# A recurrence's inner steps redistributed: accumulating transfers, a spectrum computed twice, a new order of steps

## The chip, the cores and the metric

One core of a Trainium2 chip runs the whole program. The metric is the device time of one execution in microseconds (us). The core's engines work side by side, each through its own queue in order: TensorE (PE, matrix products into PSUM), VectorE (DVE), ScalarE (ACT, functions from tables), GpSimd (POOL, which also issues transfers) and SyncE (SP, which only issues transfers). Both kinds of transfers run on the core's 16 DMA engines.

## The reference

An image of 256 x 256 pixels with 128 channels in float32 goes through four layers; each takes a group norm of the image and adds its result to it. The first layer is an attention along rows, the third a triangle product, the fourth a 3x3 convolution. The change lies in the second, a recurrence with 64 complex channels:

```python
mag = jnp.sqrt(Ar ** 2 + Ai ** 2 + 1e-08)
scale = 0.95 * jax.nn.sigmoid(mag) / (mag + 1e-08)
Ar = Ar * scale
Ai = Ai * scale
...
Bx_r = Br * x_r - Bi_ * x_i
Bx_i = Br * x_i + Bi_ * x_r
inp_r = delta[..., :c] * input_gate[..., :c] * Bx_r
inp_i = delta[..., c:] * input_gate[..., c:] * Bx_i
...
def step(h_state, _):
    h_r, h_i = h_state
    Ah_r = Ar * h_r - Ai * h_i
    Ah_i = Ar * h_i + Ai * h_r
    return ((fg_r * Ah_r + inp_r, fg_i * Ah_i + inp_i), None)
...
(h_r, h_i), _ = jax.lax.scan(step, h0, None, length=T)
```

A and B are the two-dimensional Fourier transforms of 7x7 complex filters, forget gate, input gate and delta come from products of the normalised image with 128x128 weights, and T is 16. The step is linear with a 2x2 matrix for each pixel and channel, so that 16 steps have a closed form in the matrix's trace and determinant.

## The kernel before, in words

The stages run one after another: statistics, attention, recurrence (the function `recurrence`), triangle, convolution. The recurrence takes the image in 64 blocks of 1024 pixels. A block's tiles have 128 partitions (64 channels for each of two halves of the block) and are 512 wide (`thin`) or 2 x 512 wide (`wide`, real and imaginary part). For every block these steps run, each a small function named in the table `order`:

- `ld` loads the pixels twice in two layouts (`xf`, `xc`) and the rows of both filters' transforms (`hs`, eight small transfers) on SP's queue.
- `za` and `zb` make the spectra of A and B from `hs` on TensorE into PSUM; `zd`, `zf`, `zi` are the three gates' products. They share two PSUM buffers of two banks each (tag `z`).
- `a2` squares the spectrum of A on ScalarE, `m2` adds the two squares with TensorE by means of the identity into PSUM (tag `s`), `lm`, `mg`, `lb`, `iv`, `sg` and `s` make the factor `scale` from it. `zaa` copies the spectrum into the SBUF tile `ar`.
- `f`, `ig`, `ae`, `al_`, `q`, `qg` are the gates' functions; `p0`, `p1`, `bx` and `v` make the input term.
- `ff`, `pf`, `t`, `d_`, `D_` give determinant and trace; `tq`, `dn`, `tr` and `u` with 2, 4, 8, 16 double the number of steps; `pf`, `t`, `u2` and `t1` are products on POOL, `u4` and `u8` on VectorE.
- `y0` and `y1` multiply `ar` with `v` on VectorE, `av` combines them with TensorE (PSUM tag `y`), `yf` and `yb` finish that part. `ac1` and `ac2` add both results onto `xc` by transfers that accumulate, issued by POOL.
- `ev_` and `bn` sum the result and its square over each block on ScalarE (into `parts`) for the next group norm; `st` writes `xc` to memory on POOL's queue.

`order` lists each step with a lag: in round `it` the step works on block `it - lag`, so that up to five blocks are in work at once. `pin` (`keep_in_program_order`) holds a step behind the instruction traced before it on its engine; the loads of `ld` are not pinned. Tiles are taken from rings of `bufs` buffers, and a buffer is written again only when its readers are done. Helpers record most instructions, so many steps have one line in the profile: L995 is a VectorE tensor-tensor, L1001 a scalar-tensor-tensor, L998 a product on POOL, L55 ScalarE, L61 TensorE.

After the last block 56 short products keep TensorE going (`warm`), `parts` is reduced, and the triangle stage begins with `tap_products` (nine 128x128 products of the convolution's taps with its dense weights) and `group_affine` (scale and shift of the group norm from the sums).

Of the kernel before, what the change touches and what calls it, by code (L numbers as in the profile page):

```python
# [31 lines left out]
class Kernel:  # L32
# [50 lines left out]
    def group_affine(self, pool, psum, stats, tag, shift=None, mv=None, busy=8):  # L83

        nc, V = self.nc, self.nc.vector
        pin = self.tc.keep_in_program_order
        pm = psum.tile([P, 2], F32, name=f"pm{tag}", tag="gn")
        d, v, mg, sd = (pool.tile([P, 1], F32, name=f"{n}{tag}") for n in ("gd", "gv", "mg", "sd"))
        if mv is None:
            mv = pool.tile([P, 2], F32, name=f"mv{tag}")  # L90
            V.tensor_reduce(mv, stats, AX.X, ALU.add)
            self.keep_busy(psum, busy)
            pin(self.mm(pm, self.g4n, mv))
            self.keep_busy(psum, 3)
# [812 lines left out]
    def recurrence(self, x1T, x2T, HD_, stats1, shift1, stats2, shift2):  # L907
# [7 lines left out]
        with ExitStack() as c:  # L915
# [58 lines left out]
            def load(b):  # L974
# [7 lines left out]
                d["hs"] = self.first_rows if b == 0 else self.row_transforms(io.tile([P, 2, HC], F32, name="hs", bufs=2), HD_, b)  # L982
# [34 lines left out]
            def total(d, name, pairs):  # L1017

                n = len(pairs)
                z = d[name] = ps.tile([P, n, 512], F32, name=name, tag="y" if n == 2 else "s", bufs=1 if n == 2 else 2)  # L1020
# [25 lines left out]
            def ab(d): halves(d, wide(d, "az"), "d", "zd", AF.Identity)  # L1046
            def ae(d): act(wide(d, "ex"), d["az"], AF.Sigmoid, scale=-1.0)
            def al_(d): act(d["ex"], d["ex"], AF.Ln, bias=1e-37)
            def q(d): stt(wide(d, "q", 2), d["ex"], -1.0, d["az"], MUL, MAX)

            def sg(d): act(d["mag"], d["mag"], AF.Sigmoid)
            def s(d): tt(thin(d, "s", 3), d["mag"], d["inv"], MUL)
# [3 lines left out]
            def ig(d): halves(d, wide(d, "ig"), "i", "zi", AF.Sigmoid)  # L1056
            def zaa(d): act(wide(d, "ar", 2), d["za"].rearrange("p r i v -> p i r v"), AF.Copy)
# [3 lines left out]
            def t(d): gt(thin(d, "t", 3), d["fs"], d["ar"][:, 0], MUL)  # L1061
            def d_(d): tt(thin(d, "d"), d["m2"][:, 0], d["ff"], MUL)
# [26 lines left out]
            def u4(d): tt(thin(d, "u4"), d["u2"], d["tr4"], MUL)  # L1089
            def tq8(d): squared(d, "tq8", "tr4")  # L1090
            def dn8(d): squared(d, "dn8", "dn4", 2)
# [3 lines left out]
            def xa(d): stt(thin(d, "g", 2), d["t"], -2.0, d["u8"], ADD, MUL)  # L1095
# [32 lines left out]
            def ev_(d): statistic(d, 0, AF.Identity)  # L1128
            def bn(d): statistic(d, 1, AF.Square, shifted=True)
            def st(d):  # L1130
                b = d["b"]
                for half in range(2):
                    dst = x2T[:, b * 1024 + half * 512:b * 1024 + (half + 1) * 512]
                    pin(nc.gpsimd.dma_start(dst.rearrange("(r c) n -> c r n", c=HC), d["xc"][half * HC:(half + 1) * HC]))
            def ld(d): load(d["b"])
# [16 lines left out]
            warm = ps.tile([P, 1, 512], F32, name="warm", tag="s")  # L1152
            for _ in range(56):
                pin(self.mm(warm[:, 0, :P], self.ident, self.cmat))
            red = wp.tile([P, 2, 2], F32, name="partsum")
            V.tensor_reduce(red, parts, AX.X, ADD)
            pr = ps.tile([P, 2], F32, name="partps", tag="s")
            for ri in range(2):
                self.mm(pr[ri * HC:(ri + 1) * HC], fold, red[:, :, ri])
            V.tensor_copy(stats2[:, :, 0], pr)  # L1160

    def triangle(self, x2T, x3T, znT, prodD, rs2D, rs3D, stats2, shift2, stats3, shift3, prepare):
# [368 lines left out]
    def tap_products(self, ps):  # L1531

        W, V = self.weights, self.nc.vector
        kt, wd = W["kt"], W["wd"]
        pb = ps.tile([P, 2], F32, name="cpb", tag="gn")
        self.mm(pb[:, 0:1], wd, W["bv"])
        V.tensor_copy(W["bw"], pb[:, 0:1])
        for t in range(3):
            pk = ps.tile([P, 3, P], F32, name="cpk")
            for n in range(3):  # L1540
                self.mm(pk[:, n], kt[:, 3 * t + n, :], wd)
            V.tensor_copy(kt[:, 3 * t:3 * t + 3, :], pk)
# [178 lines left out]
    def run(self, ctx):  # L1721
# [10 lines left out]
        stats["2"] = const.tile([P, 2, 1], F32, name="stats2")  # L1732
        shift2 = const.tile([P, 1], F32, name="shift2")
# [87 lines left out]
```

## Time and profile before

| What | us |
|---|---|
| median of 3 runs | 4684.48 |
| range of the runs | 4682.95 to 4684.81 |
| profiled execution | 4678.77 |
| its span | 4677.0 |
| first and last `za` in it | 1649.8 and 2909.7 |
| `partsum`, the recurrence's last reduction | 2973.1 |

Over the whole span TensorE is busy 97%, VectorE 80%, ScalarE 71% and POOL 45%. These are averages over four different stages. Busy time of TensorE is modelled, and the durations of matrix products overlap, so their sum is more than the time that they take; the same holds to a smaller degree for VectorE and ScalarE, whose instructions overlap by some 70 to 90 ns. Where a step's cost in a full queue is wanted, the distance from its start to the next start is the better number.

### The profile page before, as it was taken

The page shows a single profiled execution, that of the slowest core. Times are in us where ns is not written, and L with a number is a line of the kernel's source. Part 1 is how long each engine was busy: PE and PEld are TensorE (multiplying, and loading weights), DVE is VectorE, ACT ScalarE, POOL GpSimd, SP SyncE. Part 2 cuts the span into 40 slices and gives each one's busy share as a digit, 9 for nine tenths or more (in the row PEclk, how much of TensorE's full clock was granted, in tenths as well). Part 3 has the DMA queues.
Part 4 walks back from the last instruction along what each step waited for, and adds up shares of the span by engine and source line. Part 5 has one row for each costly group of instructions (what it writes and reads, how often), then busy time and mean ns, then how long its engine had stood idle before and what let it go on. Part 6 is the DMA issues. An engine that isn't in the chain of part 4 may idle for free. (4 is left out here: it accounts for less than half of the span.)

```text
span 4677.0 us, 79571 instructions
## 1 busy us (share of the span) xinstructions
PE 4521.0 (97%) x30445; PEld 2600.4 (56%) x30445; DVE 3750.3 (80%) x4827; ACT 3333.0 (71%) x5173; POOL 2101.5 (45%) x1379
## 2 busy tenths in 40 slices
PE   8999999999999989999999999899999999999999
PEld 2444555555555533333333333456999973379999
DVE  7776777777777679999999999787666677789885
ACT  7556888888888889999999999798443454442110
POOL 1333555555555547667666667333231245520000
PEclk9999999999999999999999999999999999999999
DMA  9892122222222235555555555576667758955432
GB/s 316 327 357 110 54 83 82 87 82 82 85 88 82 69 88 132 134 133 130 134 130 133 136 129 126 184 253 246 243 222 262 251 211 327 360 208 174 135 114 72
DMA packets 219655, 768.19 MB, mean 164 GB/s; under 512 B 58443, under 2 KB 60620, under 8 KB 178926
## 3 DMA queue, kind: packets, MB, share of 16 engines
q1 hardware_dynamic: 153976, 465.15, 29.2%
q0 software_dynamic: 65232, 297.90, 22.2%
q8 instruction: 244, 4.00, 0.3%
q14 instruction: 139, 1.14, 0.1%
q10 hardware_dynamic: 64, 0.00, 0.0%
HBM read 431.32 MB, written 265.55 MB: 149 GB/s over the span
## 5 line engine op out<-in xcount | busy, mean ns | idle before, releaser
L629 DVE TENSOR_TENSOR e<-sc,bT 128x1024 f32<-128x1024 f32 x512 | 613.8, 1220 | 255.8 <-PE sc L61 254.8
L629 POOL TENSOR_TENSOR ks<-e 128x1024 f32<-128x1024 f32 x256 | 602.4, 2371 | 443.2 <-PE nd L61 429.9
L55 ACT ACTIVATE e<-e 128x1024 f32<-128x1024 f32 x512 | 539.3, 1053 | 40.3 <-DVE e L629 30.7
L61 PE MATMUL m<-U,v 128*128 128x128 f32 x4608 | 514.8, 275 | 1.5 <-DVE v L1656 1.5
L61 PEld LDWEIGHTS m<-U,v 128*128 128x128 f32 x4608 | 514.6, 192 | 1.7 <-DVE v L1656 1.7
L61 PEld LDWEIGHTS z<-wf,zt 128*128 128x128 f32 x4096 | 462.6, 192 | 53.6 <-DVE LR L1169 28.0
L61 PE MATMUL z<-wf,zt 128*128 128x128 f32 x4096 | 474.8, 277 | 5.6 <-DVE LR L1169 5.5
L1169 DVE TENSOR_TENSOR LR<-z,sg 128x512 f32<-128x512 f32 (+1 forms) x323 | 270.0, 867 | 165.3 <-ACT sg L55 165.3
L1169 POOL TENSOR_TENSOR zt<-zt,df 128x512 f32<-128x512 f32 x127 | 161.5, 1271 | 423.2 <-ACT df L55 423.2
L55 ACT ACTIVATE sg<-z 128x512 f32<-128x512 f32 (+1 forms) x323 | 160.7, 509 | 243.7 <-PE z L61 241.4
L61 PE MATMUL sc<-proj 32*128 32x256 f32 x4096 | 300.5, 404 | 3.2 <-DVE e L629 2.4
L998 POOL TENSOR_TENSOR fs<-f 128x512 f32<-128x512 f32 x64 | 176.4, 2756 | 275.1 <-DVE f L995 251.1
L61 PEld LDWEIGHTS sc<-proj 32*128 32x128 f32 x4096 | 188.5, 185 | 161.8 <-PE px L61 94.8
L61 PE MATMUL nd<-e,proj 128*32 128x256 f32 x4096 | 273.7, 385 | 2.6 <-DVE og L629 2.6
L55 ACT ACTIVATE dn<-dn 128x512 f32<-128x512 f32 x384 | 237.9, 620 | 12.5 <-DVE dn L629 8.5
L1696 ACT COPY m4s<-m 128x512 f32<-128x512 f32 x32 | 18.7, 585 | 304.3 <-PE m L61 304.3
L61 PE MATMUL z<-LR 128*128 128x256 f32 x1024 | 225.5, 383 | 7.5 <-DVE LR L1169 7.5
L998 POOL TENSOR_TENSOR u<-t,tr 128x512 f32<-128x512 f32 x64 | 225.6, 3525 | 11.9 <-DVE tr L1001 10.1
L998 POOL TENSOR_TENSOR t<-t,v 128x1024 f32<-128x1024 f32 x63 | 206.9, 3285 | 50.2 <-DVE t L995 49.5
L1706 POOL DMA_DIRECT2D out_dram<-ys x32 | 37.0, 1157 | 420.9 <-DVE ys L1704 420.9
L61 PEld LDWEIGHTS z<-LR 128*128 128x128 f32 x1024 | 196.6, 192 | 35.5 <-DVE LR L1169 8.3
L1169 POOL TENSOR_TENSOR zt<-ga,zt 128x1024 f32<-128x1024 f32 x62 | 144.7, 2353 | 118.5 <-DVE ga L1169 118.5
(430 smaller groups left out, 10738.4 us busy)
## 6 DMA issues: line engine op xcount, KB each, us to landing
zt<-znT SPq DMA_DIRECT2D x96, 1024.0 KB
zt<-x2T SPq DMA_DIRECT2D x64, 1024.0 KB
xin<-in_x_dram SPq DMA_DIRECT2D x48, 1024.0 KB
xr<-x3T SPq DMA_DIRECT2D x46, 768.0 KB
x1T<-x POOLq DMA_DIRECT2D x64, 512.0 KB, 5.0
xf<-x1T SPq DMA_DIRECT2D x64, 512.0 KB
xc<-x1T SPq DMA_DIRECT2D x128, 256.0 KB
x2T<-xc POOLq DMA_DIRECT2D x128, 256.0 KB, 3.7
```

Of the source, the lines that this page charges most:

```text
L55: return self.nc.scalar.activation(out, in_, func, bias=bias, scale=scale, **kw)
L61: return self.nc.tensor.matmul(out, lhsT, rhs, start=start, stop=stop)
L629: pin = lambda f: lambda *a, **k: tc.keep_in_program_order(f(*a, **k))
L998: pin(nc.gpsimd.tensor_tensor(out, a, b_, op))
L1169: pin = lambda f: lambda *a, **k: tc.keep_in_program_order(f(*a, **k))
L1696: nc.scalar.copy(m4, m[4])
L1706: nc.gpsimd.dma_start(out[row:row + 8].rearrange("r p t c -> p (r t) c"), ys.rearrange("p g k t c -> p (g k t) c"))
```

## The change

The sum of the two squares (`m2`) is made by a transfer that accumulates one half of `a2` onto the other (by VectorE for the first block); `lm` and `d_` read it in SBUF. `ev_` becomes a transfer that accumulates `xc` onto one tile `summed`, except in the last block; `summed` is reduced once at the end. The spectrum of A is made a second time (`zc`), two rounds after `za`, and `y0` and `y1` read it in PSUM; `zaa` copies only the real part. `u4` goes from VectorE to POOL, and so does the last block's `t1`. `st` goes from POOL's queue to SP's. Short products (`f1`, `f2`, three a round) stand beside the two spectra of A. Buffers of several tiles change in number: `hs` has three instead of two; PSUM tag `s` one instead of two, with one bank for the short products. The lags and the order of all steps are new. `tap_products` runs in round 2 of the recurrence, pinned, and the group means for the next norm come from the same place as the sums (`means2`).

```diff
+            spare = ps.tile([P, 512], F32, name="spare", bufs=1)
+
+            def awake(n):
+                for _ in range(n):
+                    pin(self.mm(spare[:, :P], self.ident, self.cmat))
+
             parts = wp.tile([P, 2, 2, NB], F32, name="parts2")
+            V.memset(parts, 0.0)
+            summed = io.tile([P, 2, 512], F32, name="summed", bufs=1)
+            nc.gpsimd.memset(summed, 0.0)
...
+            folded = wp.tile([P, HC], F32, name="folded")
+            V.tensor_tensor(folded, self.g4n[:, :HC], self.g4n[:, HC:], ADD)
...
-                d["hs"] = self.first_rows if b == 0 else self.row_transforms(io.tile([P, 2, HC], F32, name="hs", bufs=2), HD_, b)
+                d["hs"] = self.first_rows if b == 0 else self.row_transforms(io.tile([P, 2, HC], F32, name="hs", bufs=3), HD_, b)
...
-            def a2(d): act(rows(wide(d, "a2")), d["za"], AF.Square)
-            def m2(d): total(d, "m2", [[(self.ident, d["a2"][:, 0]), (self.ident, d["a2"][:, 1])]])
-            def lm(d): act(thin(d, "mag"), d["m2"][:, 0], AF.Ln, bias=1e-8)
+            def a2(d): act(rows(wide(d, "a2", 2)), d["za"], AF.Square)
+            def m2(d):
+                if d["b"]:
+                    pin(nc.gpsimd.dma_start(d["a2"][:, 0], d["a2"][:, 1], accum_op=ADD))
+                else:
+                    tt(d["a2"][:, 0], d["a2"][:, 0], d["a2"][:, 1], ADD)
+            def lm(d): act(thin(d, "mag"), d["a2"][:, 0], AF.Ln, bias=1e-8)
...
-            def zaa(d): act(wide(d, "ar", 2), d["za"].rearrange("p r i v -> p i r v"), AF.Copy)
+            def zaa(d): act(thin(d, "ar", 2).rearrange("p (r v) -> p r v", v=N), d["za"][:, :, 0], AF.Copy)
...
-            def t(d): gt(thin(d, "t", 3), d["fs"], d["ar"][:, 0], MUL)
-            def d_(d): tt(thin(d, "d"), d["m2"][:, 0], d["ff"], MUL)
+            def t(d): gt(thin(d, "t", 3), d["fs"], d["ar"], MUL)
+            def d_(d): tt(thin(d, "d"), d["a2"][:, 0], d["ff"], MUL)
...
-            def u4(d): tt(thin(d, "u4"), d["u2"], d["tr4"], MUL)
+            def u4(d): gt(thin(d, "u4"), d["u2"], d["tr4"], MUL)
...
-            def y0(d): tt(wide(d, "y0"), d["ar"], both(d["v"][:, 0]), MUL)
-            def y1(d): tt(wide(d, "y1"), d["ar"], both(d["v"][:, 1]), MUL)
+            def zc(d): spectrum(d, 0, "zc")
+            def turned(d, n, k):
+                v = d["v"][:, k].rearrange("p (r v) -> p r v", v=N).unsqueeze(2).to_broadcast([P, 2, 2, N])
+                tt(rows(wide(d, n)), d["zc"], v, MUL)
+            def y0(d): turned(d, "y0", 0)
+            def y1(d): turned(d, "y1", 1)
...
-            def t1(d): (tt if last(d) else gt)(wide(d, "t1"), both(d["t"]), d["v"], MUL)
+            def t1(d): gt(wide(d, "t1"), both(d["t"]), d["v"], MUL)
...
-            def ev_(d): statistic(d, 0, AF.Identity)
+            def ev_(d):
+                if last(d):
+                    statistic(d, 0, AF.Identity)
+                else:
+                    pin(nc.gpsimd.dma_start(summed, d["xc"], accum_op=ADD))
...
-                    pin(nc.gpsimd.dma_start(dst.rearrange("(r c) n -> c r n", c=HC), d["xc"][half * HC:(half + 1) * HC]))
+                    pin(nc.sync.dma_start(dst.rearrange("(r c) n -> c r n", c=HC), d["xc"][half * HC:(half + 1) * HC]))
+            def f1(d): awake(2)
+            def f2(d): awake(1)
...
-                (e_, 3), (ld, 0), (za, 0), (u4, 2), (zb, 1), (a2, 0), (av, 2), (t, 1), (p1, 1), (zaa, 0), (m2, 0),
-                (tq8, 2), (al, 3), (zd, 0), (ev_, 4), (lD, 2), (q, 1), (yf, 2), (p0, 1), (tq2, 1), (dn2, 1), (tr2, 1),
-                (eD, 2), (tr8, 2), (lm, 0), (dn8, 2), (mg, 0), (ab, 0), (t1, 3), (qg, 1), (lb, 0), (tq16, 2), (bx, 1),
-                (ac1, 3), (iv, 0), (u8, 2), (yb, 3), (zf, 0), (sg, 0), (tq4, 1), (v, 1), (y1, 1), (f, 0), (xa, 2),
-                (D_, 1), (s, 0), (u2, 1), (ac2, 3), (tr4, 1), (ae, 0), (fs_, 0), (zi, 0), (y0, 1), (ff, 0), (pf, 0),
-                (xb, 2), (ig, 0), (be, 2), (al_, 0), (bn, 4), (d_, 0), (dn4, 1), (st, 4),
+                (ld, 0), (f1, 0), (za, 0), (a2, 0), (f2, 2), (zc, 2), (m2, 0), (bx, 2), (zaa, 0), (ac2, 4), (u2, 2), (dn8, 3),
+                (pf, 1), (v, 2), (tq16, 3), (xb, 3), (t, 1), (tq4, 2), (y1, 2), (zd, 0), (ae, 1), (dn2, 2), (lD, 2),
+                (ab, 0), (y0, 2), (be, 3), (zb, 1), (ff, 1), (eD, 2), (av, 2), (tq2, 1), (lm, 0), (mg, 0), (e_, 3),
+                (tr4, 2), (al, 3), (zi, 0), (p0, 1), (dn4, 2), (lb, 0), (p1, 1), (al_, 1), (iv, 0), (u4, 2), (yf, 2),
+                (ig, 0), (t1, 3), (d_, 1), (tq8, 2), (yb, 3), (zf, 0), (tr2, 1), (q, 1), (f, 0), (tr8, 2), (qg, 1),
+                (ac1, 3), (u8, 2), (sg, 0), (s, 0), (D_, 1), (bn, 4), (xa, 2), (ev_, 4), (st, 4), (fs_, 0),
...
+                if it == 2:
+                    self.tap_products(ps)
...
+            awake(56)
+            V.tensor_reduce(parts[:, 0, :, 0:1], summed, AX.X, ADD)
             red = wp.tile([P, 2, 2], F32, name="partsum")
             V.tensor_reduce(red, parts, AX.X, ADD)
...
+            pr = ps.tile([P, 2, 2], F32, name="partps", tag="s", bufs=1)
+            for n, m in enumerate((folded, fold)):
+                for ri in range(2):
+                    pin(self.mm(pr[ri * HC:(ri + 1) * HC, n], m, red[:, :, ri]))
+            awake(3)
+            means = self.means2
+            V.tensor_copy(means, pr[:, 0])
+            V.tensor_copy(stats2[:, :, 0], pr[:, 1])
...
-                self.tap_products(ps0)
-                ab, mg, _ = self.group_affine(wp, ps0, stats2, "2", shift=shift2, busy=0)
+                ab, mg, _ = self.group_affine(wp, ps0, stats2, "2", shift=shift2, means=self.means2)
```

More of the change, by code (lines that the diff above doesn't have):

```diff
@@ L79, in load, with group_affine @@
         return t
-    def group_affine(self, pool, psum, stats, tag, shift=None, mv=None, busy=8):
+    def group_affine(self, pool, psum, stats, tag, shift=None, mv=None, busy=8, means=None):
         nc, V = self.nc, self.nc.vector
         pin = self.tc.keep_in_program_order
-        pm = psum.tile([P, 2], F32, name=f"pm{tag}", tag="gn")
+        pm = None if means is not None else psum.tile([P, 2], F32, name=f"pm{tag}", tag="gn")
         d, v, mg, sd = (pool.tile([P, 1], F32, name=f"{n}{tag}") for n in ("gd", "gv", "mg", "sd"))
         if mv is None:
[L90 to L94, printed above, removed]
+            if means is None:
+                mv = pool.tile([P, 2], F32, name=f"mv{tag}")
+                V.tensor_reduce(mv, stats, AX.X, ALU.add)
+                self.keep_busy(psum, busy)
+                pin(self.mm(pm, self.g4n, mv))
+                self.keep_busy(psum, 3)
+            else:
+                pm = means
             V.tensor_tensor(d, pm[:, 0:1], shift, ALU.add)
@@ L1019, in total @@
                 n = len(pairs)
-                z = d[name] = ps.tile([P, n, 512], F32, name=name, tag="y" if n == 2 else "s", bufs=1 if n == 2 else 2)
+                z = d[name] = ps.tile([P, n, 512], F32, name=name, tag="y" if n == 2 else "s", bufs=1)
                 for i, terms in enumerate(pairs):
@@ L1045, in zd, with ab, q, s @@
             def zd(d): gate(d, "d")
-            def ab(d): halves(d, wide(d, "az"), "d", "zd", AF.Identity)
+            def ab(d): halves(d, wide(d, "az", 2), "d", "zd", AF.Identity)
             def ae(d): act(wide(d, "ex"), d["az"], AF.Sigmoid, scale=-1.0)
             def al_(d): act(d["ex"], d["ex"], AF.Ln, bias=1e-37)
-            def q(d): stt(wide(d, "q", 2), d["ex"], -1.0, d["az"], MUL, MAX)
+            def q(d): stt(wide(d, "q"), d["ex"], -1.0, d["az"], MUL, MAX)
             def sg(d): act(d["mag"], d["mag"], AF.Sigmoid)
-            def s(d): tt(thin(d, "s", 3), d["mag"], d["inv"], MUL)
+            def s(d): tt(thin(d, "s"), d["mag"], d["inv"], MUL)
             def zf(d): gate(d, "f")
@@ L1055, in zi, with ig @@
             def zi(d): gate(d, "i")
-            def ig(d): halves(d, wide(d, "ig"), "i", "zi", AF.Sigmoid)
-            def zaa(d): act(wide(d, "ar", 2), d["za"].rearrange("p r i v -> p i r v"), AF.Copy)
+            def ig(d): halves(d, wide(d, "ig", 2), "i", "zi", AF.Sigmoid)
+            def zaa(d): act(thin(d, "ar", 2).rearrange("p (r v) -> p r v", v=N), d["za"][:, :, 0], AF.Copy)
             def fs_(d): tt(d["f"], d["f"], both(d["s"]), MUL)
@@ L1082, in tq2, with dn2, u2 @@
             def tq2(d): squared(d, "tq2", "t")
-            def dn2(d): squared(d, "dn2", "d", 2)
+            def dn2(d): squared(d, "dn2", "d")
             def tr2(d): stt(thin(d, "tr2"), d["d"], -2.0, d["tq2"], MUL, ADD)
-            def u2(d): gt(thin(d, "u2", 2), d["t"], d["tr2"], MUL)
+            def u2(d): gt(thin(d, "u2"), d["t"], d["tr2"], MUL)
             def tq4(d): squared(d, "tq4", "tr2")
@@ L1088, in tr4, with dn8 @@
             def tr4(d): stt(thin(d, "tr4"), d["dn2"], -2.0, d["tq4"], MUL, ADD)
-            def u4(d): tt(thin(d, "u4"), d["u2"], d["tr4"], MUL)
+            def u4(d): gt(thin(d, "u4"), d["u2"], d["tr4"], MUL)
             def tq8(d): squared(d, "tq8", "tr4")
-            def dn8(d): squared(d, "dn8", "dn4", 2)
+            def dn8(d): squared(d, "dn8", "dn4")
             def tr8(d): stt(thin(d, "tr8"), d["dn4"], -2.0, d["tq8"], MUL, ADD)
@@ L1094, in tq16, with xa @@
             def tq16(d): squared(d, "tq16", "tr8")
-            def xa(d): stt(thin(d, "g", 2), d["t"], -2.0, d["u8"], ADD, MUL)
+            def xa(d): stt(thin(d, "g"), d["t"], -2.0, d["u8"], ADD, MUL)
             def last(d): return d["b"] == NB - 1
@@ L1127, in statistic @@
                     act(junk, d["xc"][:, ri], func, accum_out=parts[:, k, ri, b:b + 1], **({"bias": shiftc[:, ri:ri + 1]} if kw else {}))
-            def ev_(d): statistic(d, 0, AF.Identity)
+            def ev_(d):
+                if last(d):
+                    statistic(d, 0, AF.Identity)
+                else:
+                    pin(nc.gpsimd.dma_start(summed, d["xc"], accum_op=ADD))
             def bn(d): statistic(d, 1, AF.Square, shifted=True)
@@ L1151, in recurrence @@
                         step(D[it - lag])
-            warm = ps.tile([P, 1, 512], F32, name="warm", tag="s")
-            for _ in range(56):
-                pin(self.mm(warm[:, 0, :P], self.ident, self.cmat))
+            awake(56)
+            V.tensor_reduce(parts[:, 0, :, 0:1], summed, AX.X, ADD)
             red = wp.tile([P, 2, 2], F32, name="partsum")
             V.tensor_reduce(red, parts, AX.X, ADD)
[L1157 to L1160, printed above, removed]
+            pr = ps.tile([P, 2, 2], F32, name="partps", tag="s", bufs=1)
[6 more added lines that the diff above has]
+            V.tensor_copy(stats2[:, :, 0], pr[:, 1])
     def triangle(self, x2T, x3T, znT, prodD, rs2D, rs3D, stats2, shift2, stats3, shift3, prepare):
@@ L1531, in tap_products @@
     def tap_products(self, ps):
-        W, V = self.weights, self.nc.vector
+        W, pin = self.weights, self.tc.keep_in_program_order
         kt, wd = W["kt"], W["wd"]
-        pb = ps.tile([P, 2], F32, name="cpb", tag="gn")
-        self.mm(pb[:, 0:1], wd, W["bv"])
-        V.tensor_copy(W["bw"], pb[:, 0:1])
+        pb = ps.tile([P, 2], F32, name="cpb", tag="s", bufs=1)
+        pin(self.mm(pb[:, 0:1], wd, W["bv"]))
+        pin(self.nc.vector.tensor_copy(W["bw"], pb[:, 0:1]))
         for t in range(3):
-            pk = ps.tile([P, 3, P], F32, name="cpk")
+            pk = ps.tile([P, 3, P], F32, name="cpk", tag="s", bufs=1)
             for n in range(3):
-                self.mm(pk[:, n], kt[:, 3 * t + n, :], wd)
-            V.tensor_copy(kt[:, 3 * t:3 * t + 3, :], pk)
+                pin(self.mm(pk[:, n], kt[:, 3 * t + n, :], wd))
+            pin(self.nc.vector.tensor_copy(kt[:, 3 * t:3 * t + 3, :], pk))
     def transformed_taps(self, late):
@@ L1732, in run @@
         stats["2"] = const.tile([P, 2, 1], F32, name="stats2")
+        self.means2 = const.tile([P, 2], F32, name="means2")
         shift2 = const.tile([P, 1], F32, name="shift2")
```

## The prediction

> **What bounds the kernel now.** I read the page's slices first, then the engines by stretches, then the recurrence's groups, waits and order of time. The blocks of the recurrence fill 1650 to 2974 us. Inside it:
>
> ```profile
> core 0: us, PE busy (x) PEld busy (x) DVE busy (x) ACT busy (x) POOL busy (x), PEclk, DMA share, GB/s
> 2200.00:2400.00 200.00, 189.24 (x574) 66.21 (x572) 198.61 (x250) 198.91 (x339) 136.30 (x80) 1.00 0.56 133
> ```
>
> ScalarE and VectorE are both over 99% busy and TensorE's granted clock is 1.00, so no single engine can be relieved with profit; POOL has about 6 us free per block. ScalarE does not appear at all in the list of who waited for whom. One block lasts 20.16 us: ScalarE's Square of `za` starts at 2108.41 and, ten blocks on, at 2310.01. ScalarE's queue of work is therefore the bound, and VectorE is just behind. The groups that the change touches (busy, mean ns, idle before):
>
> ```profile
> L998 POOL TENSOR_TENSOR u<-t,tr 128x512 f32<-128x512 f32 x10 | 35.4, 3544 | 0.3
> L998 POOL TENSOR_TENSOR t<-t,v 128x1024 f32<-128x1024 f32 x10 | 33.0, 3300 | 7.0 <-DVE t L995 7.0
> L998 POOL TENSOR_TENSOR fs<-f 128x512 f32<-128x512 f32 x10 | 27.8, 2784 | 41.6 <-DVE f L995 41.6
> L995 DVE TENSOR_TENSOR y<-ar,v 128x1024 f32<-128x1024 f32 x20 | 24.4, 1222 | 0.3
> L995 DVE TENSOR_TENSOR q<-q,ig 128x1024 f32<-128x1024 f32 x10 | 15.4, 1542 | 0.0
> L998 POOL TENSOR_TENSOR t<-fs,ar 128x512 f32<-128x512 f32 x10 | 13.0, 1300 | 0.1
> L1134 POOL DMA_DIRECT2D x2T<-xc x20 | 13.0, 656 | 0.0
> L55 ACT ACTIVATE x2q<-xc 128x512 f32<-128x512 f32 x20 | 12.5, 627 | 0.3
> L55 ACT ACTIVATE ar<-za 128x1024 f32<-128x1024 f32 x10 | 10.1, 1013 | 0.0
> ```
>
> The odd thing is POOL: one 128x512 product takes 1.30 us and another of the same size 3.54. The order of time explains it:
>
> ```profile
> 2215.49 4.48 POOL L998 TENSOR_TENSOR u<-t,tr 128x512 f32<-128x512 f32 x1
> ...
> 2215.88 1.22 DVE L995 TENSOR_TENSOR q<-q,ig 128x1024 f32<-128x1024 f32 x1
> 2217.01 0.68 DVE L995 TENSOR_TENSOR u<-u,tr 128x512 f32<-128x512 f32 x1
> 2217.62 1.22 DVE L995 TENSOR_TENSOR yf<-yf,g 128x1024 f32<-128x1024 f32 x1
> 2218.75 1.21 DVE L1001 SCALAR_TENSOR_TENSOR v<-q,bx 128x1024 f32<-128x1024 f32 x1
> ...
> 2920.45 1.65 POOL L998 TENSOR_TENSOR u<-t,tr 128x512 f32<-128x512 f32 x1
> 2920.88 2.30 DVE L995 TENSOR_TENSOR q<-q,ig 128x1024 f32<-128x1024 f32 x1
> ```
>
> While VectorE runs instructions with both inputs in SBUF (`q`, `u`, `yf`), POOL's product stands; it ends with `v`, whose second input `bx` is in PSUM, so its own work is about 1.25 us. The last two lines are the opposite case: POOL got in first and VectorE's `q*ig` took 2.30 instead of 1.22. [...]
>
> **The change, part by part, per block.** Steps are counted start to start, since the instructions overlap.
>
> *ScalarE.* `ev_` (two reductions of `xc` with their reads) goes: in the order of time they take 2211.55 to 2212.92, 1.37 us. `zaa` halves: from 0.91 start to start to 0.52, the step of the other 512-wide ones, -0.39. `lm` reads SBUF instead of PSUM: 575 against 624 ns for `mag<-mag`, +0.04. The two table loads stay (the new order still goes once to the logarithms and once to the sigmoids). 20.16 - 1.37 - 0.39 + 0.04 = 18.44 us.
>
> *VectorE.* Its own work in one undisturbed block is `v` to `v`, 2199.10 to 2218.75: 19.65 us in 25 instructions; the rest to 20.16 is `q*ig` being locked out (1542 against 1219 ns) and small waits. `u4` leaves: 0.61. `y0` and `y1` now read `zc` from PSUM in a broken pattern. No row shows this: below, `v` with one PSUM input (1211) against `y` (1222) gives -0.01 each; above, `p` with PSUM in rows of 256 (740) against a plain 512 (684) gives +0.11 for twice the width. I take +0.05 each. `d_` from SBUF instead of PSUM is equal (680 against 684). 19.65 - 0.61 + 0.1 = 19.14 us: the new bound.
>
> *TensorE.* By starts, before: three gates of 1.77, `pxb` 2.77, `av` 3.6, `bx` 3.6, `m2` 1.9, and `za` with `zb` together 1.3 to 2.1 = 18.7 or more. `m2` goes (-1.9); `zc` comes at about 0.95 (as `za` alone, 2909.55 to 2910.50, before `zb`), and `za`, `zb`, `zc` no longer run side by side (+0.4); three 128-wide fillers add about 0.6. Sum 18.75, so TensorE hides only 0.4 us below VectorE.
>
> *A ring through both.* `xb`'s third product waits for `tq16` on ScalarE, `zd` stands behind it, and `ab` on ScalarE waits for `zd`. From `tq16`'s end: 0.95 + 2.0 = 3.0; from `ab` on to the next `tq16`: 18.44 less `tq4`, `ae`, `dn2`, table load and `lD` (3.9) = 14.5. Together 17.5, under the bound. The second spectrum takes TensorE's buffers in turn (`za`, `zd`, `zi` one, `zc`, `zb`, `zf` the other), and each earlier reader (`zaa`, `ab`, `ig`; `y0`, `p1`, `f`) stands ahead in the order; a stall would come only if `y0` or `p1` is late, and then VectorE is the late one anyway.
>
> *POOL.* The transfers `m2` (0.66, as another of 256 KB, to 0.9) and `ev_` (0.9) come, the two `st` (1.3) leave for SP, `u4` comes. [...] By the mean of the rows `u4` costs POOL up to 3.5 us: 14.1 + 3.5 + 1.7 - 1.3 = 18.0. [...] The new order forms two such stretches: `v`, `y1`, `y0`, `be` (1.24 + 1.14 + 1.14 + 0.6 = 4.1 us) for `u2`, `pf`, `t` (3.9), and `p0`, `p1`, `yf` (3.8) for `u4`, `t1` (1.25 + 2.37, the mean of the attention's 128x1024 product on POOL = 3.6). They fit with 0.2 us each, so some blocks miss. I charge half of what is lost today in `q*ig`, 0.16: 19.3 us.
>
> *Behind POOL's waits.* `m2` on POOL waits for `a2`, and `ac2`, `u2`, `pf`, `t` are queued behind it; `tq2` on ScalarE and then `tr2` wait for `t`. With ScalarE 0.7 us short of work it runs early: `a2` can end 2.5 us ahead of `v`, the two issues take 1.7, so POOL is in place. `lm` wants `m2` landed some 6 us after its issue; 512 KB land in 4.4 to 7.2, 256 KB of `x2T` in 3.7. Uncovered, a late landing would stop ScalarE, which has the 0.7 to give.
>
> *DMA.* One 512 KB accumulation keeps the 16 engines 2.65 us (47.3% of 5.6 us in a stretch of the drain that holds one alone). `ev_` adds 2.65 and `m2` 1.33 to today's 0.56 x 20.16 = 11.3: 15.3 of 19.3, 79%. [...] Queue by queue (39.0 and 17.2% now, `st` being 1.8 us) POOL's would only go to about 51%[...]. Landings get longer; `ac2` has 6.2 us behind `ac1` where 20 of 63 waited at about 4.5.
>
> A `yf` buffer is written again some 10 us after `ac2` is issued; a landing beyond 10 would stop VectorE.
>
> *SP.* 8 `hs` at 0.80, `xf` 0.34, two `xc` 1.35, and now `st` 1.35 = 9.4 us per block, under 19. `hs` in three buffers is released by `zc`, as now by `zb`, early in the block before its use.
>
> *Ends.* `tap_products` leaves the gap between stages: there the chain from `partsum` to `pc` takes 7.1 us (2973.08 to 2980.21), of which `pm` waited until 2978.36. About 3.5 goes; the reduction of `summed` (1024 elements) adds 1.1; inside the fill the nine products and three copies cost 0 to 3, I take 1.5. The accumulation for the last block but one no longer stands in ScalarE's tail, -1. The longer lags (`v`, `y0`, `y1`, `be`, `ff`, `tr4`, `d_` one round later) move 5.9 us of VectorE's work from the fill to the drain; the drain has holes on VectorE (`t` at 2954.16 came after POOL had been idle 6.4 us), so I take 0, with 5 either way. Together -2.
>
> **Sum.** 20.16 - 19.3 = 0.86 us over 60 full blocks (63 starts follow one another, the first few were shorter already) = 52, and 2 at the ends: -54. The profiled execution took 4678.8 (span 4677.0), so 4625; the median lies 5.7 above it, so 4630.
>
> **Rivals.** *POOL misses its stretches.* One lock-out of 1.1 us (2.30 against 1.22) in most blocks gives 19.14 + 0.6 to 1.0 = 19.7 to 20.15, that is 4654 to 4683. For it: margins of 0.2 us. Against: a miss repeats only if POOL stays late.
>
> *SP puts `st` before the loads (slower).* `st` is pinned and waits for `ac2` landed; if the next block's loads stand behind it, there is a ring: `za` 0.95, `a2` 1.06, `m2` 0.8, `ac2` issue to landing 5.0, `st` 1.35, `xf` and `xc` 1.7, eight `hs` 6.7, their landing about 3 (estimate, from 3.0 to 5.4 for the loads and stores of `xc`) = 20.6 us, +0.44 x 63 = +28: about 4710, more if the fuller DMA engines stretch it. It decides from the point where `hs` is issued over 6 us after its buffer is free. Against: the loads are not pinned, and today they do run ahead, with `hs` between `xf` and `xc`.
>
> *POOL's ring (slower).* If `u2`, `pf`, `t` keep 3.54, 2.78 and 1.30, then `tq2` to the end of the next `a2` on ScalarE (18.44 less the 7.1 of `zaa`, `dn8`, `tq16`, `tq4`, `ae`, `dn2`, a table load, `lD`, `ab`, `eD` that stand between = 11.3) plus `m2`, `ac2` (1.7) plus these 7.6 is 20.6 us: again about 4710.
>
> *The order does not do what it says*: TensorE's 18.75 with 0.5 us of waits would be 19.3, inside my forecast.
>
> **How the numbers follow.** Forecast (19.05 to 19.55) 0.68, 4607 to 4646; missed stretches 0.15, 4646 to 4690; the two rings 0.17, 4694 to 4760. The low end is 19.02 (`y` at its lower bound, no lock-out) with -6 at the ends. The range 4606 to 4690 holds some 0.8. Within 0.2% (9 us, about what a measurement can tell) lies only the far part of the missed stretches, 0.05; faster 0.78, slower 0.17.
>
> **What would show it.** A block of 19.1 to 19.5 us; VectorE over 98% busy, ScalarE about 95%; `y` at 1.21 to 1.33; `u4` and `u2` near 1.3; `q*ig` near 1.22; `za` never waiting for `hs`. Wrong if ScalarE waits for `t` or `m2`, if SP's loads wait behind `st`, or if `y` takes over 1.4.

## The result, and the profile after

The changed kernel takes 4721.86 us (median of 4 runs, 4712.70 to 4727.87) against 4684.65 for the kernel before on the same chip: 1.0082 times as long, 95% interval [1.007, 1.0094]. It is slower, by 37 us, and the prediction said 54 faster. The profiled execution took 4727.87 us, its span 4725.7.

First the slices by engine, for the same stretch as before (columns: sum, TensorE, its weight loads, VectorE, ScalarE, POOL, granted clock, DMA share, GB/s):

```profile
2200.00:2400.00 200.00, 200.00 (x627) 74.48 (x626) 187.18 (x235) 182.54 (x297) 111.37 (x89) 0.96 0.80 168
```

ScalarE came down from 198.91 to 182.54, as was meant; POOL came down from 136.30 to 111.37 although it got a product more; DMA rose from 0.56 to 0.80. But VectorE, which was to be the new bound, is at 187.18, TensorE at 200.00, and the granted clock is no longer 1.00. The groups that answer to those of before (busy, mean ns, idle before). The lines of the program have moved: L1009, L1015 and L1012 are what L995, L1001 and L998 were.

```profile
L1012 POOL TENSOR_TENSOR t<-t,v 128x1024 f32<-128x1024 f32 x10 | 23.8, 2378 | 0.0
L1009 DVE TENSOR_TENSOR y<-zc,v 128x1024 f32<-128x1024 f32 x19 | 22.4, 1218 | 0.3
L1012 POOL TENSOR_TENSOR u<-t,tr 128x512 f32<-128x512 f32 x10 | 19.4, 1940 | 0.0
L1012 POOL TENSOR_TENSOR fs<-f 128x512 f32<-128x512 f32 x10 | 19.1, 1912 | 0.0
L1012 POOL TENSOR_TENSOR u<-u,tr 128x512 f32<-128x512 f32 x10 | 16.6, 1663 | 31.4 <-DVE tr L1015 31.4
...
L1009 DVE TENSOR_TENSOR q<-q,ig 128x1024 f32<-128x1024 f32 x10 | 12.1, 1213 | 0.0
...
L55 ACT ACTIVATE ar<-za 128x512 f32<-128x512 f32 x10 | 5.9, 586 | 0.0
```

Every product on POOL is shorter than before (3300 to 2378, 3544 to 1940, 2784 to 1912), and VectorE's `q*ig` is no longer locked out (1542 to 1213). The part of the change that deals with POOL and VectorE works. The loss is on TensorE. The waits from 1800 to 2900 us name it:

```profile
engine line waited for: us in total, times, longest us
...
ACT az L55 <- PE zd L61: 98.2, 54, 2.6
...
DVE v L1015 <- PE bx L61: 69.4, 53, 2.1
```

VectorE's `v` waits for `bx` in nearly every block, ScalarE's `az` for `zd`. A steady block (from one Square of `za` to the next) takes either 19.53 or 21.23 us. Here is TensorE at the start of a long one (start, us, engine, line, operation, count):

```profile
2185.26 0.71 PE L61 MATMUL spare<-cmat,ident 128*128 128x128 f32 x4
2185.90 1.13 PE L61 MATMUL za<-ev,hs 14*128 14x512 f32 x4
2186.96 0.49 PE L61 MATMUL spare<-cmat,ident 128*128 128x128 f32 x2
2187.39 1.13 PE L61 MATMUL zc<-ev,hs 14*128 14x512 f32 x4
2188.45 1.58 PE L61 MATMUL bx<-p,scaledr 128*128 128x512 f32 x2
2189.82 1.91 PE L61 MATMUL bx<-p,scaledn 128*128 128x512 f32 x2
2191.53 1.46 PE L61 MATMUL bx<-p,scaledi 128*128 128x512 f32 x2
2192.83 1.02 PE L61 MATMUL bx<-p,scaledr 128*128 128x512 f32 x2
```

The products of `bx`, all alike, take 1.58, 1.91 and 1.46 us, and then 1.02. The slices of the same moment, with the clock in the third column from the right, say why:

```profile
2188.00:2188.50 0.50, 0.50 (x5) 0.05 (x1) 0.50 (x2) 0.50 (x2) 0.00 (x0) 1.00 0.71 147
2188.50:2189.00 0.50, 0.50 (x4) 0.26 (x3) 0.50 (x2) 0.47 (x2) 0.00 (x0) 0.99 1.00 238
2189.00:2189.50 0.50, 0.50 (x2) 0.30 (x1) 0.50 (x2) 0.50 (x3) 0.00 (x0) 0.50 1.15 287
...
2191.00:2192.00 1.00, 1.00 (x2) 0.35 (x2) 0.85 (x1) 1.00 (x3) 1.00 (x3) 0.50 0.56 189
2192.00:2192.50 0.50, 0.50 (x2) 0.12 (x1) 0.00 (x0) 0.50 (x2) 0.50 (x2) 0.60 1.07 184
2192.50:2193.00 0.50, 0.50 (x3) 0.26 (x2) 0.00 (x0) 0.50 (x1) 0.50 (x2) 1.00 1.07 188
```

For about 3.4 us (2189.0 to 2192.4) the granted clock is 0.50, directly after two spectra of 14 rows that stand together, and although TensorE is never idle. That costs 3.4 x 0.5 = 1.7 us, just what the long blocks are longer by.

Two spectra together are not enough for that, however. In the kernel before, `zb` stands directly behind `za` in 18 of the 64 blocks, and the clock stays at 1.00 there:

```profile
2183.82 1.13 PE L61 MATMUL za<-ev,hs 14*128 14x512 f32 x4
2184.77 1.20 PE L61 MATMUL zb<-ev,hs 14*128 14x512 f32 x4
2185.89 1.13 PE L61 MATMUL av<-y,ident 128*128 128x512 f32 x2
```

The slices of the same moment:

```profile
2182.65:2186.06 3.41, 3.41 (x12) 1.03 (x11) 3.41 (x5) 3.38 (x5) 2.04 (x1) 1.00 0.85 211
2186.06:2189.47 3.41, 3.41 (x8) 1.27 (x8) 3.41 (x7) 3.38 (x7) 3.28 (x4) 1.00 0.42 91
```

What differs is what stands beside them: products over 128 rows there, fillers here. How much of each stood there is counted below, in the part on why the prediction was wrong.

The profiled execution's 49 us by stretch (start of `a2` to start of `a2`, after less before):

| stretch | before | after | difference |
|---|---|---|---|
| start of the program to the first `a2` | 1651.6 | 1654.4 | +2.8 |
| first five blocks | 94.0 | 106.1 | +12.1 |
| next 58 blocks | 1169.2 | 1187.2 | +18.0 |
| last `a2` to the triangle's `pc` | 65.4 | 77.4 | +12.0 |
| `pc` to the end | 1696.8 | 1700.7 | +3.9 |

The 58 blocks at 19.53 would have been 36.5 shorter than at 20.16; the 54.5 us above that are 32 times 1.70.

### The profile page after: what moved, and what is told of

Same layout as the page of the kernel before. It is cut to its first block, busy times and chain, and to the rows that moved or that the text cites. A ratio compares the mean times of both kernels' runs of the same rounds, so it can differ in the third digit from the quotient of the medians.

```text
span 4725.7 us, 80279 instructions
## 1 busy us (share of the span) xinstructions
PE 4624.3 (98%) x30831; PEld 2665.9 (56%) x30831; DVE 3696.4 (78%) x4766; ACT 3236.9 (68%) x4921; POOL 1953.6 (41%) x1443
## 5 line engine op out<-in xcount | busy, mean ns | idle before, releaser
L1728 ACT COPY m4s<-m 128x512 f32<-128x512 f32 x32 | 18.7, 586 | 304.6 <-PE m L61 304.6
L1055 POOL DMA_DIRECT2D a<-a x63 | 53.9, 855 | 400.2 <-ACT a L55 393.2
L61 PE MATMUL av<-y,ident 128*128 128x512 f32 x384 | 193.3, 612 | 0.8 <-DVE y L1009 0.8
L1012 POOL TENSOR_TENSOR u<-u,tr 128x512 f32<-128x512 f32 x64 | 106.0, 1656 | 203.4 <-DVE tr L1015 203.4
```

The source lines that it names most:

```text
L61: return self.nc.tensor.matmul(out, lhsT, rhs, start=start, stop=stop)
L1012: pin(nc.gpsimd.tensor_tensor(out, a, b_, op))
L1055: pin(nc.gpsimd.dma_start(d["a2"][:, 0], d["a2"][:, 1], accum_op=ADD))
L1728: nc.scalar.copy(m4, m[4])
```

## The experiments

Theory: two bare spectra side by side bring the clock down, and the changed kernel is bound by TensorE. Rivals: TensorE is full whatever its clock; or VectorE, POOL or a transfer sets the block. Each edit is against the changed kernel unless another is named, and each ratio is to the kernel before on the same chip. A "filler" is one of the steps `f1` (two short products) and `f2` (one).

**The second spectrum apart from the first.** Only the place of `zc` in TensorE's order changes:

```diff
-                (ld, 0), (f1, 0), (za, 0), (a2, 0), (f2, 2), (zc, 2), (m2, 0), (bx, 2), (zaa, 0), ...
+                (ld, 0), (f1, 0), (za, 0), (a2, 0), (f2, 2), (m2, 0), (bx, 2), (zc, 2), (zaa, 0), ...
```

> The changed kernel with the second spectrum of A (zc) moved on TensorE from beside za to behind bx; the short products stay. Theory A (clock): za, zc and the short products beside them are a stretch of 3.2 us in which TensorE's products have 14 rows or are short; [...] the granted clock falls to 0.50 for 3.4 us and the block takes 21.2 instead of 19.5 us. Apart, no half-clock stretches are left, every block takes 19.5 us and the time is 4722 - 33 x 1.7 = about 4665. Rival B (the clock falls because TensorE is never idle): the half-clock stretches stay wherever the spectra stand, 4715 to 4728.

Measured: 4662.06, ratio 0.9964 [0.9952, 0.9977] to the kernel before. All blocks take 19.52.

```profile
2200.00:2400.00 200.00, 200.00 (x657) 72.54 (x655) 197.92 (x247) 189.32 (x306) 116.53 (x93) 1.00 0.84 178
```

The instructions are the same, TensorE is as full as in the changed kernel, and the clock is 1.00. By the two ratios 1.2% of the time, 55 us, hang on where four short products stand. It also shows what TensorE's work is at full clock: 19.52 per block, not 18.75.

**No fillers.** The steps `f1` and `f2` are taken out; the spectra stay together.

```diff
-                (ld, 0), (f1, 0), (za, 0), (a2, 0), (f2, 2), (zc, 2), (m2, 0), ...
+                (ld, 0), (za, 0), (a2, 0), (zc, 2), (m2, 0), ...
```

> The changed kernel without the short products f1 and f2 beside the two spectra. TensorE's own sum falls from 19.5 to 18.45 us. Theory A[...]: the bare spectra (2.1 us side by side) are weaker still and the half clock comes in as many blocks or in every one, 18.45 + 1.0 to 1.7 = 19.5 to 20.15 us, 4665 to 4702. Theory A, if the short products only lengthen the weak stretch: no half clock, VectorE bounds at 19.1 to 19.3, 4640 to 4652. Rival B (the clock falls because TensorE is never idle): TensorE gets holes, the half clock goes, 4640 to 4652 as well, but then the run with zc apart keeps its half clock.

Measured: 4785.81, ratio 1.0224 [1.0205, 1.0243], slower than any expectation. Of the 58 steady blocks 51 now have half clock, 33 of them for 3.4 us and 18 for 6.8:

```profile
2206.74 1.67 PE L61 MATMUL zc<-ev,hs 14*128 14x512 f32 x4 [0.48 <-ACT f L55]
2208.34 2.08 PE L61 MATMUL bx<-p,scaledr 128*128 128x512 f32 x2
2210.21 1.91 PE L61 MATMUL bx<-p,scaledn 128*128 128x512 f32 x2
2211.91 1.91 PE L61 MATMUL bx<-p,scaledi 128*128 128x512 f32 x2
2213.62 1.22 PE L61 MATMUL bx<-p,scaledr 128*128 128x512 f32 x2
```

So the fillers, in the place of waits, do hold the clock up (0.96 in 2200 to 2400 with them, 0.91 without), only not enough. TensorE also had to wait beside the spectra here (0.38 us before `za`, 0.48 for `f`), so this run alone does not say whether idle time or thin rows did it.

**Thin fillers.** The same fillers over the 14 rows that a spectrum uses instead of 128:

```diff
-            def awake(n):
+            def awake(n, rows_of=P):
...
-                    pin(self.mm(spare[:, :P], self.ident, self.cmat))
+                    pin(self.mm(spare[:, :P], self.ident[:rows_of], self.cmat[:rows_of]))
...
-            def f1(d): awake(2)
-            def f2(d): awake(1)
+            def f1(d): awake(2, 2 * KS)
+            def f2(d): awake(1, 2 * KS)
```

> The changed kernel with the short products f1 and f2 made over 14 rows instead of 128: the same number of products, the same columns and the same 19.5 us for TensorE, the spectra side by side as in the change. Theory A [...]: the short products no longer count, half clock in nearly every block, 4760 to 4790 as without them. Rival (every moment with a product running counts as busy): as the changed kernel, 4712 to 4728.

Measured: 4770.11, ratio 1.0172 [1.0148, 1.0197], with half clock in 48 of the 58 blocks.

```profile
2200.00:2400.00 200.00, 196.69 (x593) 74.54 (x593) 177.70 (x224) 172.62 (x282) 102.46 (x83) 0.90 0.77 162
```

As many instructions, with 14 rows, hardly hold the clock: 0.90 here, 0.96 with 128 rows, 0.91 without fillers. They lasted a little less too (285 against 309 ns), and TensorE had a hole of 0.33 us before `zc`; that could be the cause as well, and this run alone does not tell the two apart.

**Apart, and no filler.** From the version with the spectra apart, the taps back at the triangle's start and one filler (below), the last filler is taken out:

```diff
-                (ld, 0), (f1, 0), (za, 0), (a2, 0), (m2, 0), (bx, 2), (zc, 2), (zaa, 0), ...
+                (ld, 0), (za, 0), (a2, 0), (m2, 0), (bx, 2), (zc, 2), (zaa, 0), ...
```

> The same version (spectra apart, taps back) with no filler at all. Theory 'it is two 14-row spectra within one stretch that drop the clock, and one alone does not': granted clock stays at 1.00 in 2200 to 2400, blocks 19.30 (VectorE's own), total within 5 of 4638. Rival 'every bare spectrum drops it': half clock for 3.4 us in many blocks, TensorE back at 100% busy, blocks of 19.3 to 21, total 4660 to 4740. In between: the idle 0.9 us of TensorE per block lies next to za, so that only some blocks drop, 4640 to 4660.

Measured: 4628.52, ratio 0.9886 [0.987, 0.9903]; blocks of 19.18.

```profile
2200.00:2400.00 200.00, 196.14 (x607) 66.99 (x605) 198.85 (x251) 193.10 (x313) 118.64 (x95) 1.00 0.88 182
```

TensorE is less busy than in the changed kernel (196.14 against 200.00) and keeps the full clock. A bare spectrum by itself left the clock at 1.00 here, even with TensorE waiting 0.39 us before it. Against the version with one filler it gains 0.12 us a block besides. With the filler POOL met VectorE's `ff` (867 ns against 717 here); why POOL comes later with it, no run shows.

**One spectrum only.** `zaa` copies the whole spectrum again, `y0` and `y1` read it in SBUF, and `zc` is gone:

```diff
-            def zaa(d): act(thin(d, "ar", 2).rearrange("p (r v) -> p r v", v=N), d["za"][:, :, 0], AF.Copy)
+            def zaa(d): act(wide(d, "ar", 3), d["za"].rearrange("p r i v -> p i r v"), AF.Copy)
...
-            def y0(d): turned(d, "y0", 0)
-            def y1(d): turned(d, "y1", 1)
+            def y0(d): tt(wide(d, "y0"), d["ar"], both(d["v"][:, 0]), MUL)
+            def y1(d): tt(wide(d, "y1"), d["ar"], both(d["v"][:, 1]), MUL)
```

> The changed kernel with one spectrum of A: ScalarE copies both parts of za, y0 and y1 read the copy, zc is gone (three copies in the ring instead of two); the rest of the order stays. TensorE's sum is 18.5 us. Theory A: TensorE no longer bounds and no half clock, ScalarE at 18.8 and VectorE at 19.1 to 19.3, 4640 to 4655. Rival B: TensorE has holes, the half clock goes too, same time. Rival C (POOL's ring or SP's loads bound, and TensorE only fills up): 20.2 to 20.6 us per block as now, 4710 to 4725.

Measured: 4765.90, ratio 1.0189 [1.0169, 1.0208]: a miss by over 100 us. The group and the order of time:

```profile
L1009 DVE TENSOR_TENSOR y<-ar,v 128x1024 f32<-128x1024 f32 x20 | 45.2, 2298 | 0.3
```

```profile
2198.94 1.93 POOL L1012 TENSOR_TENSOR u<-t,tr 128x512 f32<-128x512 f32 x1
2199.61 1.21 DVE L1015 SCALAR_TENSOR_TENSOR v<-q,bx 128x1024 f32<-128x1024 f32 x1
2200.80 1.30 POOL L1012 TENSOR_TENSOR fs<-f 128x512 f32<-128x512 f32 x1
2200.85 4.55 DVE L1009 TENSOR_TENSOR y<-ar,v 128x1024 f32<-128x1024 f32 x2
2202.17 2.15 POOL L1012 TENSOR_TENSOR t<-fs,ar 128x512 f32<-128x512 f32 x1
```

With `ar` in SBUF both inputs of `y` are there, and POOL's `fs` and `t` shut it out: 2298 ns instead of 1218. The second spectrum saves ScalarE half a copy, but what it is worth is this: in the changed kernel `y` reads PSUM, and both run (2214.74 to 2217.09) with POOL's `fs` and `t` at work beside them (2214.19 to 2217.47). My expectation had counted the instructions and not the stretch that POOL needs. It was wrong about the clock too, which is at 0.97 in 2200 to 2400: the steady blocks have 20 stretches of 3.4 us at half clock, with one spectrum at a time. TensorE waits 1.1 us for `y` directly behind `zb`; that this wait and the thin products act together is an estimate from their places, and no run shows it by itself.

**The sum by a transfer, alone.** The kernel before, with `ev_` as in the change and nothing else:

```diff
-            def ev_(d): statistic(d, 0, AF.Identity)
+            def ev_(d):
+                if last(d):
+                    statistic(d, 0, AF.Identity)
+                else:
+                    pin(nc.gpsimd.dma_start(summed, d["xc"], accum_op=ADD))
```

> The kernel before with one part of the change alone: ev_ by an accumulating transfer onto one tile, reduced at the end. ScalarE falls to 18.8 us. If VectorE is the next bound at 19.65 plus what POOL's products lock it out for: 19.7 to 20.1 us, 4655 to 4680 against 4679. If it is TensorE's chain at about 20: no change. If the transfer on POOL's queue delays POOL's products: slower, 4690 to 4710.

Measured: 4664.43, ratio 0.996 [0.9945, 0.9976]; nearly all blocks take 19.65, with VectorE busy for 199.65 of the 200 us. With ScalarE relieved, VectorE's 19.65 of work is the bound; about a third of the gain of the best version comes from this edit alone.

**`u4` on POOL, alone.** The kernel of the last experiment with one product moved:

```diff
-            def u4(d): tt(thin(d, "u4"), d["u2"], d["tr4"], MUL)
+            def u4(d): gt(thin(d, "u4"), d["u2"], d["tr4"], MUL)
```

> The kernel before with its sum by an accumulating transfer (block 19.65, VectorE's own work, VectorE over 99% busy) and u4 moved from VectorE to POOL, in the order of before, where y reads two SBUF inputs. By instruction counts VectorE gives up 0.61 us: block 19.04, total about 4626. [...] the order has no stretch more than before, so POOL's product costs VectorE about what it took from it (a y, q or yf of 2.3 instead of 1.22) or POOL stands longer: block 19.6 to 20.2, total 4660 to 4700.

Measured: 4785.49, ratio 1.0227 [1.021, 1.0244]; blocks of 21.88, longer than either theory gave. (In this kernel L998 is VectorE's tensor-tensor.)

```profile
L998 DVE TENSOR_TENSOR t<-u,t 128x512 f32<-128x512 f32 x9 | 21.9, 2437 | 0.0
L998 DVE TENSOR_TENSOR q<-q,ig 128x1024 f32<-128x1024 f32 x9 | 20.6, 2293 | 0.0
```

Before the move these two took 682 and 1217 ns: 19.65 - 0.61 + 1.76 + 1.08 = 21.88. `u4` took the place beside VectorE's `p` that POOL's `t` had had; `t` and then `u2` fell on instructions with two SBUF inputs, and VectorE stood. In the new order, with stretches made for it, `u4` is on POOL too and these two keep 682 and 1213 ns.

**The taps back** at the triangle's start, and nothing else:

```diff
-                if it == 2:
-                    self.tap_products(ps)
...
+                self.tap_products(ps0)
```

> The changed kernel with the products of the convolution's taps back at the start of the triangle stage. Theory A: the taps in round 2 (nine products, three copies, each waiting for the other) leave TensorE cold for 25 us in the fill and cost 12 us there, against 3 to 4 at the stage's start: about 4713, with the steady blocks unchanged. Rival: the longer fill is made by the new lags, and the time stays at 4720 to 4727.

Measured: 4708.91, ratio 1.0059 [1.0037, 1.008]. The second interval between blocks is 14.39 us instead of 26.86; the steady blocks stay as in the changed kernel. The gain is 11 us by the ratios and 13 by the medians. The two ratios' intervals overlap, so that it is the profile that shows it: the first five blocks take 94.0 us instead of 106.1, as long as in the kernel before.

**Apart, with the taps back** (the first and the last edit together):

> The changed kernel with zc behind bx and the taps' products back at the triangle's start. If both effects are what the first runs say and add up: 4662 less 10 to 13 = about 4650, every block 19.5 us with the granted clock at 1.00, TensorE without a hole. If the two share a cause (a cold TensorE in the fill that the taps bring and zc's place cures), 4660.

Measured: 4652.14, ratio 0.9941 [0.9927, 0.9954]. Blocks of 19.52, still TensorE's.

**The same with one filler fewer** (`f2` out):

> The same without f2, the short product between za and bx. Theory A: TensorE's sum is 19.1 us, under VectorE's; if the clock stays at 1.00, blocks of 19.2 to 19.4 us, some 10 to 18 us less than with f2, and TensorE gets holes. [...] half clock in part of the blocks, +1.7 us each, 4665 to 4700.

Measured: 4638.48, ratio 0.9907 [0.9891, 0.9923]. Blocks of 19.30, clock 1.00, VectorE busy for 198.85 of 200: this is the block that the prediction forecast. TensorE did not get the holes that were expected; its modelled busy time is 200.00.

**The drain.** In the changed kernel's drain VectorE waits for POOL's last product and then for the transfer of the last block but one:

```profile
3007.13 3.26 POOL L1012 TENSOR_TENSOR t<-t,v 128x1024 f32<-128x1024 f32 x1 [0.53 <-DVE t L1009]
3010.42 1.23 DVE L1009 TENSOR_TENSOR xc<-xc,t 128x1024 f32<-128x1024 f32 x1 [2.25 <-POOL t L1012]
...
3019.00 1.22 DVE L1183 TENSOR_REDUCE parts<-summed 128x2 f32<-128x1024 f32 x1 [6.09 <-DMA summed<-xc]
```

Against the version with one filler, both are undone:

```diff
-            def t1(d): gt(wide(d, "t1"), both(d["t"]), d["v"], MUL)
+            def t1(d): (tt if last(d) else gt)(wide(d, "t1"), both(d["t"]), d["v"], MUL)
...
-                if last(d):
+                if d["b"] >= NB - 2:
```

> The kernel with the second spectrum apart, the taps back and one filler (block 19.30 us, last a2 to pc 76.0) with two edits in the drain: the last block but one is summed on ScalarE instead of by the transfer onto `summed`, and the last block's t1 is VectorE's again instead of POOL's. Theory 'the drain pays for what was moved' (in the changed kernel the last reduction waited for the transfer summed<-xc till 3019.0, and VectorE waited 2.25 us for POOL's last t1 of 3.26 us): last a2 to pc falls to 71 to 74 us, total about 4635 (-2 to -5 against the version without the edits). Rival 'the drain is the longer lags alone' (v, y0, y1, be, ff, tr4, d_ a round later, 5.9 us of VectorE's work moved to the end): last a2 to pc stays within 1 us of 76, total about 4638.

Measured: 4637.92, ratio 0.9907 [0.9891, 0.9924]. The last `a2` to `pc` falls from 76.0 to 73.4, as the theory has it, but the total does not follow. In the 20 us after `pc` the clock is 0.55 here against 0.75 without the edits, and `pc` to the end is 5.3 us longer: that is where the saving went in this pair of executions. That the edits cause the lower clock is not shown: in the next pair they do not.

**Without fillers, and the drain's edits:**

> The version with the spectra apart, the taps back and no filler (4628.5, blocks 19.18), with the two edits of the drain (sum of the last block but one on ScalarE, last t1 on VectorE), which took 2.7 us off the drain of the version with one filler. If the drain's saving is kept to the end: last a2 to pc 73 instead of 76, total about 4626. If it is lost behind pc or in the spread of the runs: 4628.5 within 3, not told apart. Above 4632 would say that the sum on ScalarE delays the last blocks.

Measured: 4628.41, ratio 0.9896 [0.9879, 0.9912], not told apart from 4628.52 without the edits (last `a2` to `pc` 73.4 against 76.1, and then a clock of 0.71 against 0.65). Both beat the kernel before by 50 us or more and the changed kernel, by the ratios, by about 90.

## Why the prediction was wrong

The forecast was 54 us less, and the profiled executions differ by 49 more: 103 us apart. Of these 54.5 are the clock in the steady blocks, 30 the ends, and 13 the fuller TensorE (19.53 instead of 19.3 over 58 blocks); the rest lies before the first block and in how many blocks were counted as full.

*TensorE's sum, a term that was mis-sized.* "Sum 18.75, so TensorE hides only 0.4 us below VectorE." Read by starts in a block at full clock, the changed kernel's terms are: fillers 1.08 (forecast 0.6), `za` and `zc` 2.11 together, `bx` 3.54, `pxb` 2.67, gates 5.44, `zb` 1.06, `av` 3.63. They sum to 19.53. The old terms, as listed, add up to 18.48 with the lower end of `za` with `zb` and to 19.28 with the upper; the prediction wrote "18.7 or more" and went on with 18.7. Started from the lower end, the new sum would be 18.53, which is 1.00 too small: 0.48 in the fillers and 0.52 in the three spectra (3.17 instead of 2.65), while the other terms cancel. Carried with the upper end it would have been 19.33, no longer below VectorE's 19.3. The last rival named the full TensorE, but let it stop at the forecast.

*The clock, the step that failed most: it was put at 1.00 without a reason.* The value was read from the row of before and taken over, though the change touched just what stands ahead of the drops: it set two groups of products over 14 rows next to each other and put fillers beside them. By idle time there would be no drop at all, since TensorE is 200.00 of 200.00 busy by its records, with the clock at 0.96 over that stretch. The measurement decides: busy is not enough.

The traces also say which blocks are hit. In the changed kernel all 94 stretches of constant clock begin on one grid of 3.413 us, to within 0.01 us, and so do the 26 of the kernel before. I took every window of that grid at full clock between the sixth and the last `a2`, counting each product from its start to the next one's. In the changed kernel 33 windows hold 2.03 us or more of 14-row products, and after each the clock is 0.50 for a window; 283 hold 1.99 or less, and after none. The long block shown above is such a case: the window before its half clock, 2185.58 to 2188.99, has both spectra (2.11), 0.76 of fillers and 0.54 of `bx`. In the blocks of 19.53 a border of the grid cuts the pair.

The 14-row products alone do not decide it. In the kernel before such windows hold up to 2.075 us of them, and the clock stays at 1.00; the rest, products over 128 rows, never falls below 1.34 there. In the changed kernel the rest is 1.39 or less in the 33 windows, but with fillers in it. Where the fillers are 1.07 us of it, half clock follows at 0.31 us of other products and not at 0.34. So a filler seems to stand for less than its time (an estimate: 1.34 of full products kept the clock, 0.31 with 1.07 of fillers did not).

The other runs agree without giving a border. Half clock came in 32 of the 58 steady blocks with the fillers, in 48 with fillers over 14 rows and in 51 with none; but in the last two TensorE waited beside the spectra as well (0.33 us, and 0.38 with 0.48). How much of that is the rows and how much the waits, these runs do not separate. A wait of 0.39 us before a spectrum that stands apart left the clock at 1.00.

*The ends, forecast at -2, are +28* (the 2.8 before the first block are not the change's: that stretch varies from 1646.1 to 1654.8 between runs). The taps "inside the fill cost 0 to 3" cost about 12: they run between VectorE's copies with TensorE waiting, and the next block's products run at half speed (the clock is 0.51 in 1680 to 1700).

```profile
1684.96 1.65 PE L61 MATMUL cpk<-w2wd,w2kt 128*128 128x128 f32 x6 [8.23 <-DVE bwc L1569]
1687.27 1.65 PE L61 MATMUL cpk<-w2wd,w2kt 128*128 128x128 f32 x6 [0.65 <-DVE w2kt L1574]
...
1696.74 2.08 PE L61 MATMUL bx<-p,scaledr 128*128 128x512 f32 x2
```

TensorE stood 8.23 us before the taps, and `bx` then takes 2.08 for 1.02. The drain, "0, with 5 either way", is 12 longer. The two undone edits give back 2.7 of it. The rest may be the longer lags, of which the prediction counted 5.9 us of VectorE's work; that was not tested by itself. The 3.9 after `pc` go with a lower clock (0.65 in its first 20 us against 1.00 before), but with the taps back the clock is 1.00 there and the stretch still takes 1701.9, so their cause stays open.

*What held.* VectorE's 19.65 before is the block once ScalarE is relieved. The 19.3 of the forecast is the block with the spectra apart and one filler; with none it is 19.18, beside the 19.14 that VectorE's work alone was put at. `y` was taken at +0.05 over 1.222 and is 1.218. POOL's two stretches of VectorE with an input in PSUM opened as planned (that a product costs POOL 1.25 to 1.3 us there was the author's estimate, from the 1.30 of `t` beside `p` in the kernel before), and where an experiment lacked a stretch, VectorE paid (2298 ns for `y`, 2.23 us a block for `u4` alone); `u2` and `u4` at 1.94 and 1.66 are nearer to their own 1.25 than to the 3.54 of before, not equal to it. DMA was forecast at 79% and is 0.80, but by luck: over blocks of 20.47 us on average that is 16.4 us a block instead of 15.3, and at 19.18 the share is 0.88. SP's ring did not close: `za` never waited for `hs`. So the total of 4630 is met (4628.5) by a kernel that differs from the changed one in the place of one step, two fillers and the place of the taps. That it is met so closely is in part luck: its drain is 10.7 us longer than before, where the forecast had 0, and blocks of 19.18 and a shorter fill (87.1 us against 94.0) make up for it. For the kernel as it is, the two spectra in one window with the fillers decided.

## What to carry to other kernels

When a change adds thin products or moves them together, treat TensorE's clock as part of the cost: look at the granted clock around each such group in slices of half a microsecond, count the thin products and the waits beside them, and set thin groups between full ones before buying fillers (here the place of one spectrum took the clock from 0.96 to 1.00; three fillers a block, taken out, from 0.96 to 0.91). When work goes from one engine to another, sum the new load of every engine with both ends of each term, since the next bound may be one that you put 0.4 us under it. And a product on POOL had its price in these runs where VectorE had no instructions with an input in PSUM to run beside it: `u4` cost VectorE nothing that shows in the new order (`t` 682 ns, `q` 1213) and 2.23 us a block in the old one; count those microseconds as a resource that can be used up.

## What the runs showed of the hardware

- TensorE's clock went to 0.50 for 3.4 us with TensorE without a gap in its records, and in the run without fillers, where waits came in, for 6.8 us in 18 blocks. In the traces of the kernel before and of the changed one all its changes lie on a grid of 3.413 us.
- In the changed kernel half clock followed 33 windows of the grid with 2.03 us or more of 14-row products and none of 283 with 1.99 or less. In the kernel before up to 2.075 us of them, beside at least 1.34 us over 128 rows, left the clock at 1.00.
- The same fillers over 14 rows instead of 128 went with a clock of 0.90 instead of 0.96 in 2200 to 2400, and with a wait of 0.33 us.
- The same four products of a spectrum cost nothing in clock behind `bx` (1.00 in 2200 to 2400) and about 1 us per block on average beside the other spectrum (54.5 us over 58 blocks).
- One product of 0.61 us moved from VectorE to POOL made a block 2.23 us longer, by two lock-outs of other instructions on VectorE (682 to 2437 ns and 1217 to 2293).
- An accumulating transfer of 512 KB per block in place of two reductions on ScalarE took 0.5 us off the block (20.16 to 19.65), where VectorE stopped it, with the DMA share at 0.73.
